# A transformer block with cross-attention: row maxima spread by turning a repeated column, and the modulation with the conditions as stationary side

## The chip, the core and the metric

The kernel runs on one core of a Trainium2 chip. The metric is the device time of one execution in microseconds. The engines are TensorE (PE in the profile, with PEld for its loads of the stationary operand), VectorE (DVE), ScalarE (ACT), GpSimd (POOL) and SyncE (SP, which here only issues transfers). A matrix product has a stationary operand, which is loaded first, and a moving one, which is streamed past it; the result lands in PSUM. A "turn" is a transpose on TensorE: the data is the stationary side and an identity matrix is streamed. An f32 product appears in the profile as two matmul instructions; an f32 turn and a bf16 matmul as one.

## The reference, cut to what matters

```python
# x (16, 224, 512), cond (16, 512), ctx (16, 750, 512), all float32; 16 heads of 32
c_proj = silu(c) @ W_mod + b_mod                      # (16, 6*512)
shift_a, scale_a, gate_a, shift_m, scale_m, gate_m = split(c_proj, 6)
x_norm = ln(x) * (1 + scale_a[:, None]) + shift_a[:, None]
q, k, v = split(x_norm @ W_qkv + b_qkv, 3)            # self-attention
x = x + gate_a[:, None] * (softmax(q k' * scale) v @ W_proj + b_proj)
q_c = ln(x) @ W_qc + b_qc                             # cross-attention
k_c, v_c = split(ln(context) @ W_kvc + b_kvc, 2)
x = x + softmax(q_c k_c' * scale) v_c @ W_cproj + b_cproj
h = gelu((ln(x) * (1 + scale_m) + shift_m) @ W_mlp1 + b_mlp1) @ W_mlp2 + b_mlp2
x = x + gate_m[:, None] * h
```

The softmax subtracts each query's largest score before the exponential. The change is about how that maximum reaches the scores in cross-attention, and about the first line, the modulation.

## The kernel before

The work runs in three stages, one after the other: self-attention (to some 760 us), cross-attention (to some 2230 us) and the MLP. Each engine works through its instructions in the order of the program; every operation is recorded through a helper at line 28, so the profile's line is L28 for nearly all of them, and one goes by tile names. Three PSUM pools serve the attention stages: `sc` for scores (one buffer of four banks), `mm` for projections and turns (three buffers of a bank) and `o` for values (one buffer of a bank).

**The opening** (lines 247 to 299). The inputs and weights are fetched by transfers on SP's and ACT's queues. ACT's queue first issues five small transfers that fill `brow`, one row of 128 for every 128 biases (line 140), then `c_in` (the conditions), then two transfers of `bg`, the gates' biases. SP's queue issues the first two 1 MB parts of W_mod (`w_mod`, two buffers), the first tokens `x` and W_qkv. ACT computes `c_act` = silu, TensorE turns it, and VectorE copies it to `c_t`, which holds the 16 conditions as columns. `brow` is turned into `bcol`, whose columns are per-partition biases; VectorE adds 1 to those of the scales and scales `bqc`. `make_part(i)` (line 279) then makes one of the six parts. A gate (parts 2 and 5) has `c_t` as stationary side and 512 columns of weights moving. A shift or scale (parts 0, 1, 3, 4) has 128 by 128 blocks of weights as stationary side and the 16 columns of `c_t` moving, 16 products of two instructions, so that the result stands with the features on the partitions; VectorE adds `bcol` and writes `mod_t`. Parts 0 and 1 come before the first turns of the normalized tokens (`xn` into `xt`, where VectorE applies `mod_t`) and the first projection. Parts 2 to 5 are put into slots of self-attention's first units by a plan (`at_slot`, line 513 on): 2 and 3 in unit 1, 4 and 5 in unit 3. A part's weights are fetched when the part two before it has been used. DMA issues wait in their queue where they need something, and so does all that is behind them on the same engine.

**A cross-attention unit** (class `Unit`, lines 960 to 1072) is one sample and four heads, 64 units in all, some 22.5 us each. Scores are computed turned, with context positions on the partitions (125) and the 224 queries along the free axis, in three rounds of two chunks (`scores`, `keep`). `keep` copies scores to `pt` (ACT) and gathers the largest over chunks in `top` (VectorE). `maxima` turns `top` (f32) so that queries stand on 112 partitions and VectorE reduces it to `mc`, 8 columns of negated maxima: four heads by two halves of the queries. `split_max(nc.gpsimd, nmc, m)` (line 122) writes each as the sum of three bf16 terms into the first three columns of `nmc`, whose other columns are zero: four POOL operations.

In the next unit, after its first round of scores, `max_row` turns the eight 112 by 128 blocks of `nmc` (bf16) into a PSUM tile of `mm`, and ACT copies that to `mrow`, rows of terms. `subtract(h)` multiplies a matrix of ones with 448 columns of `mrow`, which sums the three terms and repeats the result on 125 partitions in a tile `bc` of the pool `o`; VectorE adds it to `pt` for two heads. `subtract(0)` stands after the first slot of the round (in most units half of a projection of the keys, 375 columns), `subtract(1)` in the second round. `weights(h)` then applies the exponential (ACT) and sums over positions into `acc` (POOL). One unit later still, `values` multiplies `pt` with the values, adds sums from `acc`, and `finish` (VectorE, `at`) divides. A plan of slots lays the projections, turns, norms and fetches of the next sample between these steps. After the last unit the same steps are written out among the first MLP products (line 1105 on).

Of the kernel before, what the change touches and what calls it, by code (L numbers as in the profile page):

```python
# [8 lines left out]
F32 = mybir.dt.float32  # L9
BF16 = mybir.dt.bfloat16  # L10
# [27 lines left out]
def kernel(  # L38
# [73 lines left out]

# [6 lines left out]
    nmc = const.tile([TP, HG, TC, P], BF16, name="nmc")  # L119
    nc.gpsimd.memset(nmc, 0.0)  # L120

    def split_max(engine, nm, m):

        r = small.tile(list(m.shape), F32, name="rest")
        engine.tensor_copy(nm[:, :, :, 0], m)
        engine.tensor_tensor(r, m, nm[:, :, :, 0], ALU.subtract)
        engine.tensor_copy(nm[:, :, :, 1], r)
        engine.tensor_tensor(nm[:, :, :, 2], r, nm[:, :, :, 1], ALU.subtract)
# [9 lines left out]
    for off, vec in ((o_mod, b_mod), (o_qkv, b_qkv), (o_qc, b_qc), (o_kvc, b_kvc), (o_mlp, b_mlp1)):  # L138
        rows = vec.shape[0] // P
        nc.scalar.dma_start(out=brow[off : off + rows, :], in_=vec.rearrange("(r p) -> r p", p=P))  # L140
# [113 lines left out]
    wq, wk, wv = (load_w(ws, w_qkv[:, i * H : (i + 1) * H], f"wqkv{i}") for i in range(3))  # L254
    bg = mp.tile([B, 2, H], F32, name="bg", bufs=1)
# [4 lines left out]
    c_act = mp.tile([B, H], F32, name="c_act", bufs=1)  # L260
    nc.scalar.activation(c_act, c_in, AF.Silu)
# [7 lines left out]
    ps = ps_mm.tile([P, 512], F32, name="mm")  # L269
    turn(ps[:, :nbias], brow, ident[:nbias, :nbias])  # L270
    nc.vector.tensor_copy(bcol, ps[:, :nbias])
    for i in (1, 4):
        sl = bcol[:, o_mod + i * KC : o_mod + (i + 1) * KC]
        nc.vector.tensor_scalar(sl, sl, 1.0, None, ALU.add)

    bqc = const.tile([P, KC], F32, name="bqc")
    nc.vector.tensor_scalar(bqc, bcol[:, o_qc : o_qc + KC], SCALE, None, ALU.mult)

    def make_part(i):
        w = w_part[i]  # L280
        ps = ps_mm.tile([P, 512], F32, name="mm")
        if i % 3 == 2:
            for k in range(KC):
                mm(ps[:B, :H], c_t[:, k, :], w[:, k, :], start=(k == 0), stop=(k == KC - 1))
# [3 lines left out]
        else:  # L288
            slot = (i // 3) * 2 + i % 3
            for m in range(KC):  # L290
                for k in range(KC):
                    mm(
                        ps[:, m * B : (m + 1) * B], w[:, k, m * P : (m + 1) * P], c_t[:, k, :],
                        start=(k == 0), stop=(k == KC - 1),
                    )
# [138 lines left out]
    if True:  # L434
# [70 lines left out]
        for p in range(NP):  # L505
# [15 lines left out]
            if p == 0:  # L521
                at_slot(p, 1, 0, lambda: make_part(2))
                at_slot(p, 1, 1, lambda: make_part(3))
                at_slot(p, 1, 1, lambda: load_part(4))
                at_slot(p, 1, 1, lambda: load_part(5))
                at_slot(p, 3, 0, lambda: make_part(4))
                at_slot(p, 3, 1, lambda: make_part(5))
                at_slot(p, 3, 1, load_cross)
# [18 lines left out]
        def self_scores(p, g, j, nm):  # L547
# [15 lines left out]
            split_max(nc.vector, nm, m)  # L563
# [33 lines left out]
        make_part(0)  # L597
        make_part(1)
# [212 lines left out]
    with tc.tile_pool(name="ca", bufs=2, reuse_waits="tile") as ca:  # L811
# [152 lines left out]
        class Unit:  # L964
# [39 lines left out]
            def maxima(self):  # L1004
                m = small.tile([TP, HG, TC], F32, name="mc")
# [307 lines left out]
```

## Time and profile before

| what | value |
|---|---|
| median of 3 runs | 2943.95 us (2943.93 to 2952.13) |
| profiled execution | 2940.97 us, its span 2939.2 us |
| TensorE busy | 2850.1 us, 97% of the span |
| VectorE, ScalarE, GpSimd busy | 65%, 40%, 44% |
| mean granted TensorE clock | 0.991 |
| turns of `nmc`: 512; products of `mrow` with ones in cross-attention: 128 | mean 216 ns; 355 ns |
| ACT copies to `mrow` in cross-attention: 64 | mean 906 ns |

A row of a group reads: line, engine, operation, what it writes and reads, its shape and count; then busy time in us and mean duration in ns; then the idle time of the engine just before it and what ended most of it. For TensorE the shape is rows by columns of the stationary side, then rows by columns of the moving one. The duration of one matmul includes its way through the array, so matmuls overlap, and the distance between starts says what one takes from the stream. A row of the time order reads: start, length of a merged run of instructions, engine, operation, and in brackets the idle time before. A row of waits reads: who waited for whom, total us, how often, the longest. A row of a window reads: the window, its length, for each engine busy time and count, the granted clock as a share of full speed (unrecorded before 27 us, and then shown as 1.00), the busy share of the DMA engines and GB/s.

### The profile page before, as it was taken

To read this page: it belongs to the slowest core of one execution; us is meant where nothing else is said; L and a number is where in the kernel's file an instruction comes from. 1 tells how busy PE (TensorE), PEld (TensorE's weight loads), DVE (VectorE), ACT (ScalarE), POOL (GpSimd) and SP (SyncE) were. 2 spreads that over 40 slices of the span, in tenths; PEclk is the share of its full clock that TensorE was granted. 3 is DMA by queue.
4 is the path that set the end of the run, shared out by engine and by line. 5 is a ranking of instruction groups with operands and counts; after the bars stand their busy time and mean duration, and the time that the engine had idled before them with its cause. 6 is when DMAs were issued, how large, how long until landed. Compare 5 with 4: busy or idle time off the path is not lost.

```text
span 2939.2 us, 46558 instructions
## 1 busy us (share of the span) xinstructions
PE 2850.1 (97%) x19389; PEld 1829.9 (62%) x19389; DVE 1913.6 (65%) x2688; ACT 1175.4 (40%) x1462; POOL 1296.2 (44%) x1636
## 2 busy tenths in 40 slices
PE   8999999998999999999999999999978999999999
PEld 5544444444555565555656555555545888888888
DVE  3677766676478778777787777777775643443343
ACT  1222222221466665666566656665653022112211
POOL 1022222122367666676666766666564510221021
PEclk9999999999999999999999999999989999999999
DMA  5111110100100010100101100000012101111110
GB/s 189 59 32 32 32 32 11 59 11 26 54 32 24 22 35 24 34 28 19 34 24 34 35 18 28 26 33 24 22 44 99 55 30 49 43 47 30 54 44 29
DMA packets 55383, 114.40 MB, mean 39 GB/s; under 512 B 4308, under 2 KB 4372, under 8 KB 55172
## 3 DMA queue, kind: packets, MB, share of 16 engines
q1 hardware_dynamic: 54560, 110.58, 11.7%
q8 instruction: 152, 2.49, 0.4%
q10 hardware_dynamic: 612, 0.85, 0.1%
q14 instruction: 59, 0.48, 0.1%
HBM read 89.33 MB, written 22.09 MB: 38 GB/s over the span
## 4 chain that ended last, share of the span: by engine, by line
PE 80%; DVE 8%; issue 4%; ACT 4%; POOL 3%; DMA 1%; SPq 0%; ACTq 0%; POOLq 0%; DVEq 0%
PE mm L28 46%; PE a L28 10%; PE sc L28 9%; PE o L28 8%; PE b L28 5%; ACT pt L28 3%; PE c L28 3%; DVE at L28 2%; DVE top L28 2%; POOL acc L28 1%; DVE stats L28 1%; DVE m L28 1%; DVE mc L28 1%; ACT kt L28 1%; DMA gate<-gate_d 1%
## 5 line engine op out<-in xcount | busy, mean ns | idle before, releaser
L28 POOL TENSOR_TENSOR acc<-acc,pt 125x448 f32<-125x448 f32 x512 | 584.3, 1141 | 40.2
L28 DVE TENSOR_TENSOR pt<-pt,o 125x896 f32<-125x896 f32 x384 | 394.4, 1082 | 92.0 <-PE o L28 87.0
L28 ACT COPY pt<-sc 125x1792 f32<-125x1792 f32 x192 | 317.4, 1653 | 223.3 <-DVE top L28 199.0
L28 DVE TENSOR_TENSOR top<-top,sc 125x896 f32<-125x896 f32 x320 | 346.7, 1084 | 40.6 <-PE sc L28 34.0
L28 PE MATMUL mm<-wkvc,cxt 128*125 128x512 f32 x768 | 354.4, 604 | 8.6 <-ACT kt L28 8.6
L28 POOL TENSOR_TENSOR upd<-upd,gate 112x512 f32<-112x512 f32 (+1 forms) x60 | 78.9, 1315 | 632.5 <-DVE upd L28 627.8
L28 PE MATMUL mm<-cxt,wkvc 128*128 128x375 f32 x1024 | 350.5, 484 | 2.4 <-ACT cxt L28 2.4
L28 ACT ACTIVATE pt<-pt 125x896 f32<-125x896 f32 x384 | 339.1, 955 | 12.9 <-DVE pt L28 12.2
L28 POOL TENSOR_TENSOR acc<-pt 125x448 f32<-125x448 f32 x128 | 146.5, 1144 | 382.6 <-ACT pt L28 382.6
L28 DVE RECIPROCAL at<-o 128x224 f32<-128x224 f32 x128 | 198.8, 1553 | 102.1 <-PE o L28 102.1
L28 PEld LDWEIGHTS mm<-cxt,wkvc 128*128 128x128 f32 x1024 | 190.4, 191 | 112.7 <-issue 13.3
L28 PEld LDWEIGHTS mm<-wkvc,cxt 128*125 128x125 f32 x768 | 136.5, 187 | 175.2 <-issue 153.5
L28 ACT ACTIVATE pt<-sc 112x1792 f32<-112x1792 f32 x64 | 106.6, 1665 | 343.4 <-PE sc L28 338.8
L28 POOL TENSOR_TENSOR rstd<-mv,eps 112x2 f32<-112x2 f32 (+3 forms) x93 | 17.8, 192 | 475.5 <-DVE mv L28 475.5
L28 PE MATMUL sc<-qt,kt 32*125 32x224 f32 x3072 | 201.6, 377 | 12.9 <-ACT pt L28 12.3
L28 PE MATMUL mm<-xt,wqkv 128*128 128x448 f32 x512 | 209.0, 551 | 4.7 <-DVE xt L28 4.7
L28 DVE TENSOR_REDUCE m<-sc 112x8 f32<-112x1792 f32 x64 | 129.6, 2026 | 120.3 <-PE sc L28 120.3
L28 PEld LDWEIGHTS sc<-qt,kt 32*125 32x125 f32 x3072 | 132.9, 183 | 92.6 <-issue 41.0
L28 ACT COPY mrow<-mm 128x896 bf16<-128x896 bf16 x64 | 58.0, 906 | 309.2 <-PE mm L28 309.2
L28 PE MATMUL o<-pt,vt 125*32 125x224 f32 x3072 | 158.6, 355 | 0.0
L28 PEld LDWEIGHTS mm<-xt,wqkv 128*128 128x128 f32 x512 | 92.3, 190 | 86.7 <-issue 80.9
L28 ACT COPY mx<-a 128x512 f32<-128x512 f32 x26 | 15.3, 587 | 325.0 <-POOL upd L28 306.3
(192 smaller groups left out, 4846.7 us busy)
## 6 DMA issues: line engine op xcount, KB each, us to landing
cx<-in_ctx_dram SPq DMA_DIRECT2D x96, 250.0 KB
x<-in_x_dram SPq DMA_DIRECT2D x16, 448.0 KB
x_self<-x SPq DMA_DIRECT2D x16, 448.0 KB
x<-x_self SPq DMA_DIRECT2D x16, 448.0 KB
x_cross<-x SPq DMA_DIRECT2D x16, 448.0 KB
mx<-x_cross SPq DMA_DIRECT2D x28, 256.0 KB
w<-in_L_xcond_W_mlp_dram SPq DMA_DIRECT2D x7, 1024.0 KB
xr<-x_cross SPq DMA_DIRECT2D x28, 256.0 KB
```

The source lines that it names most:

```text
L28: return lambda *args, **kw: self.tc.keep_in_program_order(f(*args, **kw))
```

## The change

In cross-attention the split into terms, `nmc`, `max_row` and `mrow` are gone. `subtract(h)` takes each f32 column of `mc` itself as the stationary side, repeated 125 times by its access pattern (a stride of zero), and turns it: four turns of 112 columns fill the tile `bc`, which VectorE adds as before. `split_max` stays for self-attention, on VectorE.

In the modulation every part now has `c_t` as stationary side (`part_rows`), with 512 columns of weights moving. For a shift or scale ACT copies the 16 rows to SBUF, and `finish_part` turns four blocks of 16 by 128 before VectorE writes `mod_t` as before. In self-attention's plan parts 3 and 4 are finished a slot or two later than their rows are made. On ACT's queue `c_in` is issued first; the transfers of `brow` and `bg` are issued behind the activation that makes `c_act`. The turn of `brow` and the additions to `bcol` come after the rows of parts 0 and 1.

```diff
...
-    nmc = const.tile([TP, HG, TC, P], BF16, name="nmc")
-    nc.gpsimd.memset(nmc, 0.0)
-
-    def split_max(engine, nm, m):
+    def split_max(nm, m):
...
-    for off, vec in ((o_mod, b_mod), (o_qkv, b_qkv), (o_qc, b_qc), (o_kvc, b_kvc), (o_mlp, b_mlp1)):
-        rows = vec.shape[0] // P
-        nc.scalar.dma_start(out=brow[off : off + rows, :], in_=vec.rearrange("(r p) -> r p", p=P))
...
         xs[b] = load_x(sa, tokens(x, b), 6)
     load_part(1)
     wq, wk, wv = (load_w(ws, w_qkv[:, i * H : (i + 1) * H], f"wqkv{i}") for i in range(3))
+    c_act = mp.tile([B, H], F32, name="c_act", bufs=1)
+    nc.scalar.activation(c_act, c_in, AF.Silu)
+    for off, vec in ((o_mod, b_mod), (o_qkv, b_qkv), (o_qc, b_qc), (o_kvc, b_kvc), (o_mlp, b_mlp1)):
+        rows = vec.shape[0] // P
+        nc.scalar.dma_start(out=brow[off : off + rows, :], in_=vec.rearrange("(r p) -> r p", p=P))
     bg = mp.tile([B, 2, H], F32, name="bg", bufs=1)
     for i in range(2):
         lo = (2 + 3 * i) * H
         nc.scalar.dma_start(out=bg[:, i, :], in_=b_mod[lo : lo + H].partition_broadcast(B))
 
-    c_act = mp.tile([B, H], F32, name="c_act", bufs=1)
-    nc.scalar.activation(c_act, c_in, AF.Silu)
 
     c_t = mp.tile([P, KC, B], F32, name="c_t", bufs=1)
     ps = ps_mm.tile([P, 512], F32, name="mm")
...
         turn(ps[:, k * B : (k + 1) * B], c_act[:, k * P : (k + 1) * P], ident[:B, :B])
     nc.vector.tensor_copy(c_t.rearrange("p k b -> p (k b)"), ps[:, : KC * B])
 
-    ps = ps_mm.tile([P, 512], F32, name="mm")
-    turn(ps[:, :nbias], brow, ident[:nbias, :nbias])
-    nc.vector.tensor_copy(bcol, ps[:, :nbias])
-    for i in (1, 4):
-        sl = bcol[:, o_mod + i * KC : o_mod + (i + 1) * KC]
-        nc.vector.tensor_scalar(sl, sl, 1.0, None, ALU.add)
-
     bqc = const.tile([P, KC], F32, name="bqc")
-    nc.vector.tensor_scalar(bqc, bcol[:, o_qc : o_qc + KC], SCALE, None, ALU.mult)
-
-    def make_part(i):
-        w = w_part[i]
+
+    def make_columns():
         ps = ps_mm.tile([P, 512], F32, name="mm")
+        turn(ps[:, :nbias], brow, ident[:nbias, :nbias])
+        nc.vector.tensor_copy(bcol, ps[:, :nbias])
+        for i in (1, 4):
+            sl = bcol[:, o_mod + i * KC : o_mod + (i + 1) * KC]
+            nc.vector.tensor_scalar(sl, sl, 1.0, None, ALU.add)
+        nc.vector.tensor_scalar(bqc, bcol[:, o_qc : o_qc + KC], SCALE, None, ALU.mult)
+
+    def part_rows(i):
+
+        ps = ps_mm.tile([P, 512], F32, name="mm")
+        for k in range(KC):
+            mm(ps[:B, :H], c_t[:, k, :], w_part[i][:, k, :], start=(k == 0), stop=(k == KC - 1))
+        if i % 3 < 2:
+            r = mp.tile([B, H], F32, name="part", bufs=2)
+            nc.scalar.copy(r, ps[:B, :H])
+            return r
+        return ps
+
+    def finish_part(i, ps):
         if i % 3 == 2:
-            for k in range(KC):
-                mm(ps[:B, :H], c_t[:, k, :], w[:, k, :], start=(k == 0), stop=(k == KC - 1))
             g = mp.tile([B, H], F32, name="gates", bufs=1)
             nc.vector.tensor_tensor(g, ps[:B, :H], bg[:, i // 3, :], ALU.add)
             nc.sync.dma_start(out=gate_d[i // 3], in_=g)
         else:
             slot = (i // 3) * 2 + i % 3
+            rows, ps = ps, ps_mm.tile([P, 512], F32, name="mm")
             for m in range(KC):
-                for k in range(KC):
-                    mm(
-                        ps[:, m * B : (m + 1) * B], w[:, k, m * P : (m + 1) * P], c_t[:, k, :],
-                        start=(k == 0), stop=(k == KC - 1),
-                    )
+                turn(ps[:, m * B : (m + 1) * B], rows[:, m * P : (m + 1) * P], ident[:B, :B])
             for m in range(KC):
                 nc.vector.tensor_scalar(
                     mod_t[:, slot * KC + m, :], ps[:, m * B : (m + 1) * B],
...
                 for i, h in enumerate(parts):
                     at_slot(p, i // 3, i % 3 // 2, h)
             if p == 0:
-                at_slot(p, 1, 0, lambda: make_part(2))
-                at_slot(p, 1, 1, lambda: make_part(3))
+                made = {}
+
+                def part(i):
+                    made[i] = part_rows(i)
+                    if i % 3 == 2:
+                        finish_part(i, made[i])
+
+                at_slot(p, 1, 0, lambda: part(2))
+                at_slot(p, 1, 1, lambda: part(3))
                 at_slot(p, 1, 1, lambda: load_part(4))
                 at_slot(p, 1, 1, lambda: load_part(5))
-                at_slot(p, 3, 0, lambda: make_part(4))
-                at_slot(p, 3, 1, lambda: make_part(5))
+                at_slot(p, 2, 0, lambda: finish_part(3, made[3]))
+                at_slot(p, 3, 0, lambda: part(4))
+                at_slot(p, 3, 1, lambda: part(5))
+                at_slot(p, 3, 1, lambda: finish_part(4, made[4]))
                 at_slot(p, 3, 1, load_cross)
             n = p + 1
             if n < NP:
...
         norm_begin(0)
         for j in range(PB):
             norms[j].all()
-        make_part(0)
-        make_part(1)
+        rows = [part_rows(i) for i in range(2)]
+        make_columns()
+        for i in range(2):
+            finish_part(i, rows[i])
         load_part(2)
         load_part(3)
         fetch(1)
...
                 self.pts.append(pt)
 
             def maxima(self):
-                m = small.tile([TP, HG, TC], F32, name="mc")
+                self.m = m = small.tile([TP, HG, TC], F32, name="mc")
                 for h in range(2):
                     ps = ps_mm.tile([P, 512], F32, name="mm")
                     for s in range(2):
...
                         ps[:TP, : 2 * TC * CP].rearrange("p (s c t) -> p s c t", s=2, c=TC),
                         AX.X, ALU.max, negate=True,
                     )
-                split_max(nc.gpsimd, nmc, m)
-
-            def max_row(self):
-                ps = ps_mm.tile([P, 1024], BF16, name="mm")
-                for s in range(HG):
+
+            def subtract(self, h):
+
+                bc = ps_o.tile([P, 512], F32, name="o")
+                for s in range(2):
                     for c in range(TC):
+
                         lo = s * N + c * TP
-                        turn(ps[:, lo : lo + TP], nmc[:, s, c, :], ident16[:TP, :TP])
-                self.row = ca.tile([P, HG * N], BF16, name="mrow", bufs=1)
-                nc.scalar.copy(self.row, ps[:, : HG * N])
-
-            def subtract(self, h):
-
-                bc = ps_o.tile([P, 512], F32, name="o")
-                mm(
-                    bc[:CP, : 2 * N], ones16[:, :CP], self.row[:, 2 * h * N : 2 * (h + 1) * N],
-                    start=True, stop=True,
-                )
+                        col = self.m[:, 2 * h + s, c : c + 1].to_broadcast([TP, CP])
+                        turn(bc[:CP, lo : lo + TP], col, ident[:TP, :TP])
                 less = bc[:CP, : 2 * N].rearrange("p (s t) -> p s t", s=2).unsqueeze(2)
                 for pt in self.pts:
                     w4 = pt[:, 2 * h : 2 * h + 2, :].rearrange("p s (k t) -> p s k t", k=2)
...
                 last.values()
             for n in range(CH):
                 st = cur.scores(n)
-                if n == 0 and prev:
-                    prev.max_row()
                 if n == 0 and last:
                     last.finish()
                 cur.keep(n, st)
...
         sc = ps_s.tile([P, HG, 512], F32, name="sc")
         prev.values()
         mlp_plain(sc[:, 0], 0)
-        cur.max_row()
         prev.finish()
         mlp_plain(sc[:, 1], 1)
         cur.subtract(0)
```

More of the change, by code (lines that the diff above doesn't have):

```diff
@@ L117 @@
         nms.append(t)
-    nmc = const.tile([TP, HG, TC, P], BF16, name="nmc")
-    nc.gpsimd.memset(nmc, 0.0)
-    def split_max(engine, nm, m):
+    def split_max(nm, m):
         r = small.tile(list(m.shape), F32, name="rest")
[L125 to L128, printed above, removed]
+        nc.vector.tensor_copy(nm[:, :, :, 0], m)
+        nc.vector.tensor_tensor(r, m, nm[:, :, :, 0], ALU.subtract)
+        nc.vector.tensor_copy(nm[:, :, :, 1], r)
+        nc.vector.tensor_tensor(nm[:, :, :, 2], r, nm[:, :, :, 1], ALU.subtract)
     o_mod, o_qkv = 0, 6 * KC
@@ L562, in self_scores @@
             )
-            split_max(nc.vector, nm, m)
+            split_max(nm, m)
         def self_weights(p, g, j, row):
```

## The prediction

> **What bounds the kernel now.** I read the page first: busy times, slices, the chain that ended last. Then TensorE's groups, shapes kept apart, and TensorE's waits inside the cross-attention stage (760 to 2160 us). Then the order of time: one unit there, and the first 30 us. Last, windows with the granted clock.
>
> ```profile
> PE 2850.1 (97%) x19389; PEld 1829.9 (62%) x19389; DVE 1913.6 (65%) x2688; ACT 1175.4 (40%) x1462; POOL 1296.2 (44%) x1636
> PE 80%; DVE 8%; issue 4%; ACT 4%; POOL 3%; DMA 1%; SPq 0%; ACTq 0%; POOLq 0%; DVEq 0%
> ```
>
> TensorE is the bound: 97% busy, 80% of the chain. So a change is priced in two coins: start-to-start time that its matmuls take from TensorE's stream, and waits of TensorE. Work on the other engines counts only where TensorE waits for it.
>
> ```profile
> L28 PE MATMUL o<-mrow,ones 128*125 128x448 bf16 x128 | 45.4, 355 | 1.0 <-ACT mrow L28 1.0
> L28 PE MATMUL mm<-ident,nmc 112*128 112x112 bf16 x512 | 37.0, 216 | 12.0 <-POOL nmc L28 12.0
> L28 PE MATMUL mm<-ident,xn 112*128 112x112 f32 x248 | 31.0, 271 | 0.0
> PE mm L28 <- POOL nmc L28: 9.6, 15, 1.1
> ```
>
> The first two groups go away; the third is nearest to what comes. The last line, from the waits in 760 to 2160, says that 15 times TensorE stood for the split maxima on POOL; the other 2.4 of the 12.0 us is one wait at 2171 to 2174.
>
> ```profile
> 1464.93 1.04 PE L28 MATMUL sc<-qt,kt 32*125 32x224 f32 x16
> 1465.90 0.57 PE L28 MATMUL mm<-ident,nmc 112*128 112x112 bf16 x8
> 1466.30 2.75 PE L28 MATMUL mm<-cxt,wkvc 128*128 128x375 f32 x8
> 1468.90 0.35 PE L28 MATMUL o<-mrow,ones 128*125 128x448 bf16 x1
> 1469.08 2.69 PE L28 MATMUL mm<-cxt,wkvc 128*128 128x375 f32 x8
> ```
>
> Starts give the price in the stream: eight turns of nmc 0.40 us (1465.90 to 1466.30), one product with ones 0.18 (1468.90 to 1469.08).
>
> ```profile
> 3.01 0.44 ACTq L28 DMA_DIRECT2D c_in<-in_cond_dram  x1
> 8.64 0.63 ACT L28 ACTIVATE c_act<-c_in 16x512 f32<-16x512 f32 x1 [0.47 <-DMA c_in<-in_cond_dram]
> 10.30 13.84 PE L28 MATMUL mm<-c_t,w_mod 128*128 128x16 f32 x64
> 23.98 3.18 PE L28 MATMUL mm<-ident,xn 112*128 112x112 f32 x16
> 27.00 6.19 PE L28 MATMUL mm<-xt,wqkv 128*128 128x448 f32 x16
> 58.63 3.61 PE L28 MATMUL mm<-w_mod,c_t 128*16 128x512 f32 x8
> 63.37 3.70 PE L28 MATMUL mm<-c_t,w_mod 128*128 128x16 f32 x32
> ```
>
> The opening is one chain: the conditions are issued sixth on ACT's queue and land after 8 us; two parts of the modulation; the turns; the first projection at 27.00. The 64 small matmuls of two parts take 13.84 us here, but 32 of one part take 3.70 at 63.37: half speed at the start. The turns agree (16 in 3.18 us; 8 in 0.93 at 95.92). From 27.00 on matmuls have their later durations.
>
> ```profile
> 66.00:69.00 3.00, 3.00 (x38) 2.11 (x41) 1.64 (x7) 0.00 (x0) 0.25 (x2) 0.82 0.91 276
> 69.00:72.00 3.00, 3.00 (x19) 1.60 (x13) 1.54 (x1) 0.00 (x0) 2.68 (x5) 0.61 0.98 373
> ```
>
> In these windows the third number from the end is the granted clock: 0.82 and 0.61 just after part 3 (63.37 to 67.07). After part 4 (80.61) it is 0.67 and 0.76 in 84 to 90; after the gate part at 58.63 it is 1.00.
>
> **The change, part by part.**
>
> *Removed, each of 64 cross units.* Eight turns of nmc, 0.40 us, and two products with ones, 2 x 0.18: 0.77 us of TensorE's stream. ACT's mrow copy (906 ns) and four POOL operations (about 218, 206, 218, 233 ns, 1.1 us in a row) leave engines with slack: TensorE waited once, 1.0 us, for mrow.
>
> *Added, each unit.* Eight f32 turns of 112 columns with a repeated column as stationary side, four in each `subtract`. Eight xn turns took 0.93 us, one alone 0.27, so the pitch is (0.93 - 0.27) / 7 = 0.095 us: eight cost 0.76, and up to 0.83 with the hand-over at each group's end. Net -0.01 to +0.06 us a unit; I take +0.03, times 64 = +2 us. The trace shows no stationary operand with a repeated element, so from below nothing is gained, and from above its load could be dearer than the stream (third rival).
>
> Here a rule speaks against the change. The Trainium skill, "TensorE: Matmul & The Clock Gate", section on the fast weight load, has that load on for 128 weights of a type that isn't FP32. The nmc turns load so (98 ns), the new ones cannot (f32 turns of xn 147 ns). By the rule each turn would pay 49 ns more: 512 x 0.049 = +25 us. By the row the loads lie under the matmuls (pitch 0.095, below either load). I take the row.
>
> *Waits that go.* The turn needs `mc`, which VectorE reduces at the end of the unit before, and comes after a half of the keys' projection (2.6 us). So nothing takes the POOL wait's place there. At 1443.19 the scores began 1.67 us before the nmc turn instead of the 0.97 above: 0.70 lost. Fifteen times: 10.5 us. What follows in such a unit leaves room: the next scores start at 1448.99, ACT released their bank at 1447.72, so 0.70 passes and the slack is still 0.6. The wait at the end, 2.4 us, I count whole, as VectorE's next work there waits for TensorE (4.7 us, at 2178.91). Sum -13, bounds -16 and, if it is taken back, 0. POOL's freed 1.1 us a unit helps where TensorE waits for `acc` (12.6 us in all); the long ones follow other POOL work, so -1 (0 to -3).
>
> *Modulation in the loop.* Part 3 and part 4 become 8 matmuls of 512 columns like the row at 58.63: 8 x 0.43 = 3.44 us, and four turns, some 0.4, against 3.70: +0.15 each, +0.3. The ACT copy (16x512, near the 0.59 of other 512-column copies) lies under other work, since finishing waits a slot. The second effect is the clock: two stretches of 3.4 us at half speed follow the narrow matmuls, at most 1.7 us each; the gate part has the new shape and no such stretch follows it. I take -3 (0 to -3.4).
>
> *The opening.* c_in is now first on ACT's queue, brow and bg are issued behind the activation. Before, brow and c_in were issued within 3 us and c_in still took 5.6 us to land, beside the 1 MB of w_mod. I take c_in in by 3, activation, turns and c_t (0.63 + 0.58 + 0.22 and hops) by 5, so part 0 starts when w_mod is in, 6.9 by the trace, instead of 10.30. Its 8 matmuls take 3.44 us at full clock, 6.9 at half; I take 5.2, to 12.1. Part 1's weights are issued at 7.15 behind x; the DMA windows add up to 2.9 MB by 12.0 and 3.1 are needed, so it starts at 13 and ends at 17.3 (between 3.44 and 5.2). Then ACT's copy 0.6, turns 0.6, mod_t 0.66, hops 0.2: 19.4. The columns of brow (0.8 us of VectorE, early before) lie beside ACT's copy. VectorE's eight xt take 3.44 as before and pace the first projection, which ends 0.75 after them, at 23.6 instead of 30.0. That is -6.4; I take -6. Bounds: -8 (12.1 and 17.3 both earlier), and -1, if the clock stays at half up to the projection (6.9 + 13.8 + 2.5 + 3.4, and a slow projection). bg is first needed at 62, brow's columns only after part 1.
>
> The second rule bears on the clock: the same page, Part 1, says that some 3.4 us of sustained activity bring full clock whatever the spacing, and Part 4 that transposes don't count as activity. By these the 64 small matmuls would have warmed the clock by 14 us, and the shape would gain nothing. The rows say otherwise: 13.8 us of 16-column matmuls ran at half, and 3.2 us of turns ended in full clock. With the rule alone the opening gains only c_in's 3.4 us, and the two stretches nothing: 5.6 us less than I sum.
>
> **Sum:** +2 - 13 - 1 + 0.3 - 3 - 6 = -20.7, against the profiled execution's 2940.97 (span 2939.2 and 1.8 around it): 2920. The median of the three runs, 2943.95, is 3 us above that execution; on its scale I say **2923 us**.
>
> **Rivals.** *The waits move.* VectorE is 77% busy in the stage and ACT's score copies wait for it; a TensorE that comes 0.7 us earlier may stand before the next scores. For: 199 us of ACT waiting for `top`. Against: the slack of 1.2 us in the unit above. Then the 13 us stay: 2937. *The opening gives nothing.* ACT must now issue seven DMAs between the activation and the copies of the modulation's rows. Before, two bg issues of about 0.4 us spanned 3.37 us on that queue; if they stand there until the 3 MB of wqkv are in (the DMA engines are full until 24 us), the copies come at about 21 and the opening is as before: 2929. *Slower:* the repeated column. If its load reads badly, all 512 turns pay. All other terms together are -22.7, so it decides from 0.044 us a turn over 0.095; at 0.25 us a turn it costs 79 us and the time is 3000. For: the kernel itself copies a repeated column into `rep` before loading it as stationary. Against: all loads in the trace go by number of columns and type, and repeated moving operands (mrow in self-attention) run at their width.
>
> **How the numbers follow.** Forecast 0.65, waits move 0.13, opening nothing 0.13, slower 0.07, and 0.02 for anything else. 0.3% is 8.8 us, about what a measurement here can tell from no change: faster is below 2935, slower above 2953. Nearly all of the forecast, most of the second rival and a third of the first are faster: 0.79; same 0.13; slower 0.08. The range takes all gains at their ends and 3 us for clock stretches at the stage's end (-34): 2910; above, it holds the first rival and reaches 2941; the column at its worst is left out. The forecast alone lies in 2911 to 2934.
>
> **What would show it.** Right: no nmc wait among TensorE's waits and about 0.97 us from the first scores to the keys' projection in every unit; new turns at a pitch near 0.095; a first projection near 20 to 24 us; clock 1.00 in 66 to 90. Wrong: pitch over 0.14; TensorE waiting longer for `pt`; the copies of the rows held behind ACT's DMA issues; the clock at half until 27 again.

## The result, and the profile after

The changed kernel takes 2922.71 us, median of four runs (2922.62 to 2924.95), where the kernel before took 2946.26 us in four runs beside them (2943.93 to 2952.13). The ratio is 0.9922, 95% interval 0.9905 to 0.9939: faster by some 0.8%. A later measurement of the same two kernels gave 2925.01 against 2941.86 us, ratio 0.9939 (0.9927 to 0.9952), so the gain is 0.6 to 0.8%. The forecast was 2923 us. The profiled execution is 2922.65 us long with a span of 2920.9 us, 18.3 less than the span before. The forecast's sum was -20.7, so on one scale, span against span, it was 2.4 us too good. It added 3 us because the profiled execution of before lies below the median of its kernel; that of the changed kernel lies at its median. So the agreement to 0.3 us is in part luck.

The changed kernel's page, busy times and the engines' shares of the chain that ended last:

```profile
PE 2847.2 (97%) x19181; PEld 1828.9 (63%) x19181; DVE 1910.2 (65%) x2688; ACT 1119.8 (38%) x1402; POOL 1241.8 (43%) x1379
PE 83%; DVE 6%; ACT 4%; issue 4%; POOL 2%; DMA 1%; SPq 0%; POOLq 0%; ACTq 0%; DVEq 0%
```

TensorE's work is the same to 3 us, ACT and POOL each lost some 55 us. The gain is not in busy time: it is in TensorE's waits and in its clock.

The new turns among TensorE's groups, and TensorE's waits in 760 to 2160 us, both of the changed kernel:

```profile
L28 PE MATMUL o<-ident,mc 112*125 112x112 f32 x512 | 76.2, 271 | 1.2 <-DVE at L28 1.2
L28 PE MATMUL mm<-ident,cx 125*128 125x125 f32 x384 | 46.7, 270 | 0.0
```

```profile
PE mm L28 <- ACT kt L28: 7.0, 15, 0.5
PE o L28 <- POOL acc L28: 6.2, 3, 3.5
PE sc L28 <- ACT pt L28: 2.3, 1, 2.3
```

The 15 waits for `nmc`, 9.6 us, are gone, and none of that size has come up elsewhere. (The waits for `acc` are 2.8 us in this window before, but only because its edge at 2160 us cuts off one of them, which now ends at 2152; over the whole span they are four and 12.6 us before, four and 12.4 after.) Two of the waits that went, in the trace of before, the first sample's and one of thirteen alike:

```profile
778.15 0.57 PE L28 MATMUL mm<-ident,nmc 112*128 112x112 bf16 x8 [1.09 <-POOL nmc L28]
1443.19 0.57 PE L28 MATMUL mm<-ident,nmc 112*128 112x112 bf16 x8 [0.63 <-POOL nmc L28]
```

The mean of 271 ns of a new turn is its way through the array; its price is read from starts.

One unit of the changed kernel in order of time, TensorE:

```profile
1451.39 1.04 PE L28 MATMUL sc<-qt,kt 32*125 32x224 f32 x16
1452.36 2.79 PE L28 MATMUL mm<-cxt,wkvc 128*128 128x375 f32 x8
1454.99 0.59 PE L28 MATMUL o<-ident,mc 112*125 112x112 f32 x4
1455.42 2.71 PE L28 MATMUL mm<-cxt,wkvc 128*128 128x375 f32 x8
```

The keys' projection follows the first scores after 0.97 us, with no turn between. Four turns take 0.43 us from the stream (1454.99 to 1455.42), 0.107 us each.

The opening of the changed kernel, TensorE and then two rows of ACT:

```profile
6.81 6.37 PE L28 MATMUL mm<-w_mod,c_t 128*16 128x512 f32 x8 [1.48 <-DMA w_mod<-in_L_xcond_W_mod_dram]
13.49 3.61 PE L28 MATMUL mm<-w_mod,c_t 128*16 128x512 f32 x8 [0.31 <-DMA w_mod<-in_L_xcond_W_mod_dram]
17.23 0.95 PE L28 MATMUL mm<-ident,part 16*128 16x16 f32 x8
20.81 6.25 PE L28 MATMUL mm<-xt,wqkv 128*128 128x448 f32 x16 [0.22 <-PE mm L28]
...
3.98 0.63 ACT L28 ACTIVATE c_act<-c_in 16x512 f32<-16x512 f32 x1 [1.49 <-DMA c_in<-in_cond_dram]
13.22 0.57 ACT L28 COPY part<-mm 16x512 f32<-16x512 f32 x1 [8.61 <-DMA bg<-in_L_xcond_b_mod_dram]
```

The first projection starts at 20.81 instead of 27.00. Both parts wait for their weights now, so that the transfers set the first 13.5 us. Part 0 runs at half speed nearly all through, part 1 at full: 6.37 us against 3.61, and the trace's record of the clock begins with full speed at 12.4 us. (The bracket of the last row names a transfer of `bg`. ACT had issued both by 10.3 us, and the copy starts 0.04 us after part 0's last matmul ends, at 13.18: it waited for TensorE.)

Windows after parts 3 and 4 of the modulation (the third number from the end is the granted clock):

```profile
66.00:69.00 3.00, 2.18 (x28) 1.45 (x28) 2.96 (x8) 1.34 (x1) 0.00 (x0) 1.00 0.03 12
84.00:87.00 3.00, 3.00 (x26) 1.76 (x23) 1.89 (x1) 0.00 (x0) 0.00 (x0) 1.00 0.23 51
```

The two stretches at half speed that followed the narrow matmuls are gone.

To see where the 18.3 us come from, matched VectorE instructions of both traces (the reductions to maxima) are set side by side; the difference of their starts, after minus before, grows like this:

| place | difference, us | step |
|---|---|---|
| first maxima of self-attention | -6.1 | opening -6.1 |
| after part 4, and to the end of self-attention | -7.8 | -1.7 |
| first maxima of cross-attention | -7.7 | hand-over of the stages +0.1 |
| first maxima of the last sample | -17.3 | -9.6 in 15 samples |
| maxima of the last sample's third unit | -20.1 | -2.8 |
| end | -18.3 | +1.8 |

Within a sample of four units the difference moves by +0.02, 0.00, +0.14 and -0.72 us, and so again in thirteen samples. In the first, where the wait before was 1.09 us, it moves by -1.03 in that unit, and in the fifteenth, where it was 0.29, by -0.35.

### The profile page after: what moved, and what is told of

It is laid out like the page before. It is cut to its first block, busy times and chain, and to the rows that moved or that the text cites. A ratio compares the mean times of both kernels' runs of the same rounds, so it can differ in the third digit from the quotient of the medians.

```text
span 2920.9 us, 45888 instructions
## 1 busy us (share of the span) xinstructions
PE 2847.2 (97%) x19181; PEld 1828.9 (63%) x19181; DVE 1910.2 (65%) x2688; ACT 1119.8 (38%) x1402; POOL 1241.8 (43%) x1379
## 4 chain that ended last, share of the span: by engine, by line
PE 83%; DVE 6%; ACT 4%; issue 4%; POOL 2%; DMA 1%; SPq 0%; POOLq 0%; ACTq 0%; DVEq 0%
PE mm L28 45%; PE a L28 10%; PE sc L28 10%; PE o L28 10%; PE b L28 5%; ACT pt L28 3%; PE c L28 3%; DVE at L28 2%; DVE top L28 1%; POOL acc L28 1%; DVE m L28 1%; ACT kt L28 1%; DMA gate<-gate_d 1%; POOL upd L28 1%; POOL xr L28 0%
## 5 line engine op out<-in xcount | busy, mean ns | idle before, releaser
L28 PEld LDWEIGHTS mm<-cxt,wkvc 128*128 128x128 f32 x1024 | 184.4, 190 | 118.3 <-issue 17.7
L28 PE MATMUL sc<-qt,kt 32*125 32x224 f32 x3072 | 203.2, 379 | 11.7 <-ACT pt L28 11.1
L28 DVE TENSOR_REDUCE mc<-mm 112x4 f32<-112x500 f32 x128 | 80.0, 666 | 87.7 <-PE mm L28 87.7
```

The costliest lines, as they stand in the source:

```text
L28: return lambda *args, **kw: self.tc.keep_in_program_order(f(*args, **kw))
```

## The experiments

The theory is the sum of the prediction: TensorE's waits for the split maxima, the shape of the modulation's products, and the early conditions, each worth its own term and independent of the rest. The rivals are those of the prediction and some for single steps.

**The modulation alone.** The kernel before with the new opening, `part_rows` and `finish_part`, and cross-attention as it was:

```diff
-        make_part(0)
-        make_part(1)
+        rows = [part_rows(i) for i in range(2)]
+        make_columns()
+        for i in range(2):
+            finish_part(i, rows[i])
```

> The opening and the modulation as changed, cross-attention as before. Theory (the two parts add up): the first maxima of self-attention 6 us earlier, no half-speed stretch near 68 and 85 us, 7.8 us gained when cross-attention starts, and there nothing more per sample: 2933 us (2929 to 2937). Rival (what the opening gains is given back at a later wait): 2941 or more, with the gain at the start of cross-attention gone by its end.

Measured: 2937.33 us in ten runs (2933.68 to 2944.34), ratio 0.9982 (0.9972 to 0.9991), a little above the range that was expected. By matched instructions the opening gave -4.1 and the two stretches -1.7; then 4.3 us were lost again where self-attention hands over to cross-attention, and the 9.6 us of waiting for `nmc` stayed.

```profile
8.37 6.30 PE L28 MATMUL mm<-w_mod,c_t 128*16 128x512 f32 x8 [2.41 <-DMA w_mod<-in_L_xcond_W_mod_dram]
15.49 3.61 PE L28 MATMUL mm<-w_mod,c_t 128*16 128x512 f32 x8 [0.82 <-DMA w_mod<-in_L_xcond_W_mod_dram]
```

The opening has the same code as in the changed kernel, where these two rows start at 6.81 and 13.49. The weights landed 1.6 and 2.0 us later in this execution, and the projection with them. The loss at the hand-over is looked at below, with the repeated run.

**Cross-attention alone.** The kernel before with the turned column, modulation and opening as they were:

```diff
-                if n == 0 and prev:
-                    prev.max_row()
...
+                        col = self.m[:, 2 * h + s, c : c + 1].to_broadcast([TP, CP])
+                        turn(bc[:CP, lo : lo + TP], col, ident[:TP, :TP])
```

> Cross-attention as changed, the opening and the modulation as before. Theory: nothing gained at the start of cross-attention, then 0.70 us in one unit of each of the 15 samples after the first, 0.15 lost in two others, some 2.5 us at the last sample: 11 us, 2930 us (2926 to 2935). The half-speed stretches near 68 and 85 us stay. Rival (the work taken from ACT and POOL is the gain): a gain in every unit alike, some 0.3 us or more, 2920 us.

Measured: 2931.26 us (2930.55 to 2932.08), ratio 0.9961 (0.9947 to 0.9975). The difference to before is +0.5 at the first maxima of cross-attention, moves by the same +0.02, 0.00, +0.14, -0.72 per sample, and takes -2.9 in the last sample. The steps in cross-attention belong to the turned column, whatever the opening does. The two halves nearly add up: 0.9982 times 0.9961 is 0.9943. The whole change was measured at 0.9922 (0.9905 to 0.9939) and later at 0.9939 (0.9927 to 0.9952). The product lies inside the second interval and just outside the first, so nothing is shown that the two halves don't hold.

**Only the order of the queue.** `c_in` first, `brow` and `bg` behind the activation, and the narrow products of the modulation as they were:

```diff
+    c_act = mp.tile([B, H], F32, name="c_act", bufs=1)
+    nc.scalar.activation(c_act, c_in, AF.Silu)
     for off, vec in ((o_mod, b_mod), (o_qkv, b_qkv), (o_qc, b_qc), (o_kvc, b_kvc), (o_mlp, b_mlp1)):
...
-        make_part(0)
-        make_part(1)
+        made = [part_products(i) for i in range(2)]
+        make_columns()
+        for i in range(2):
+            part_add(i, made[i])
```

> Before, with c_in first on ACT's queue, brow and bg behind the activation and the columns after the products of parts 0 and 1; the modulation's matmuls stay narrow. Theory (narrow matmuls don't wake the clock): they start near 6.8 and take 13.8 us at half speed as before, so the first projection starts near 23.5 to 24 (20.8 in the changed kernel, 27.0 before), the stretches near 68 and 85 us stay: 2937 to 2939 us. Rival (any 3.4 us of steady work wakes it, so the shape adds nothing): the second part at 3.7 us, the projection near 21, 2934 us.

Measured: 2943.37 us in ten runs, ratio 0.9999 (0.9990 to 1.0009). No gain, which I had not expected. The profiled execution, 2949.55 us, is the longest of the ten.

```profile
7.87 6.98 PE L28 MATMUL mm<-c_t,w_mod 128*128 128x16 f32 x32 [1.99 <-DMA w_mod<-in_L_xcond_W_mod_dram]
15.28 7.01 PE L28 MATMUL mm<-c_t,w_mod 128*128 128x16 f32 x32 [0.42 <-DMA w_mod<-in_L_xcond_W_mod_dram]
...
22.99 3.32 PE L28 MATMUL mm<-ident,xn 112*128 112x112 f32 x16 [0.41 <-DVE bcol L28]
26.10 7.54 PE L28 MATMUL mm<-xt,wqkv 128*128 128x448 f32 x16
```

Part 0 starts 2.4 us earlier than before, but part 1 stands 0.4 us for its weights and the turns 0.4 us for the columns of `brow`; both parts take 7.0 us. The projection starts 0.9 us earlier and then takes 7.54 us instead of 6.19, as full clock came only 2.6 us into it (at 28.7 us by the trace's record, against 27.0 before). At the first maxima the kernel is 0.4 us behind the one before. So with the narrow products the earlier start bought nothing that ten runs can tell. The wide ones turn it into time: from the start of part 0 to the projection it takes 18.2 us here and 14.4 in the kernel with the modulation alone, because part 1, the small turns and the 16 turns of `xn` then run at full speed.

This run also answers the rule on the clock that the prediction set aside. The Trainium skill, "TensorE: Matmul & The Clock Gate", Part 1, has some 3.4 us of sustained activity bring full clock, whatever the spacing of the matmuls. Here 14 us of 16-column products, with a gap of 0.4 us, ran at half speed to their end (7.0 us a part, against 3.70 for part 3 before), as 13.84 us of them did before. Products of 512 columns brought full clock after some 3.1 to 5.5 us (twice what part 0 is longer than 3.61, which it takes at full clock: 5.18 to 6.37 in seven executions). For this shape the measurement decides against the rule; whether the width of the moving side or the stationary one makes the difference was not separated.

**Turns of nmc later.** The kernel before, with the eight turns of `nmc` and the ACT copy to `mrow` in the middle of the keys' projection, to take away the POOL wait without the rest of the change:

```diff
+                if k == 1 and hf == 0 and between:
+                    between.pop()()
...
-                    prev.max_row()
+                    if (b, g) == units[-1]:
+                        prev.max_row()
+                    else:
+                        between.append(prev.max_row)
```

> Before, with the eight turns of nmc and ACT's copy of mrow put into the middle of the keys' projection, so that POOL's split has 1.3 us more; no work is removed. Theory (the gain in cross-attention is the wait): no wait for nmc, 0.70 us gained once in a sample, 10 to 12 us in all, 2930 to 2933 us. Rival (the gain comes of removed work): within 3 us of before, 2941 to 2945.

Measured: 3163.68 us, ratio 1.0755 (1.0739 to 1.0771); I had expected a gain. TensorE and then ACT in one unit:

```profile
1442.15 1.49 PE L28 MATMUL mm<-cxt,wkvc 128*128 128x375 f32 x4
1446.50 0.35 PE L28 MATMUL o<-mrow,ones 128*125 128x448 bf16 x1 [2.86 <-ACT mrow L28]
...
1443.99 1.65 ACT L28 COPY pt<-sc 125x1792 f32<-125x1792 f32 x1 [6.70 <-DVE top L28]
1445.54 0.91 ACT L28 COPY mrow<-mm 128x896 bf16<-128x896 bf16 x1
```

The nmc wait fell to 1.3 us, as meant. But ACT's copy to `mrow` now stands behind its copy of the scores, which itself waits for VectorE's `top`, and TensorE waits for `mrow`: 163 us in all. Units are 2.4 to 4.6 us longer, some by more than the wait itself: the clock falls in many of these gaps (the mean granted clock is 0.968). So the wait could not be had by moving the turns to this place, the only one tried: the chain runs from VectorE over POOL, TensorE and ACT back to TensorE, and what POOL gained there ACT lost. The change takes POOL and ACT out of it.

**VectorE earlier.** The kernel before, one statistic of the context's norm moved from just ahead of the late maxima to an earlier slot:

```diff
-                            b, 1 + 2 * hf, (4, 5, 5)[c] - hf, lambda b=b, hf=hf, c=c: cnorms[b + 2, hf].stats(c)
+                            b, 1 + 2 * hf, ((2, 5, 5), (3, 4, 4))[hf][c], lambda b=b, hf=hf, c=c: cnorms[b + 2, hf].stats(c)
```

> Before, with one statistic of the context norm in cross-attention's second unit of a sample moved two rounds ahead, to where VectorE stands idle 1.3 us; mc is then ready 0.9 us earlier and POOL's split too. No work is removed. Theory (what cross-attention gains is the wait for nmc): the 0.70 us of one unit in each of some 13 samples go, 9 us, 2933 us (2931 to 2936 where the clock's stretches are as before). Rival (the removed work matters): within 2 us of before.

Measured: 2940.72 us in ten runs, ratio 0.9989 (0.9980 to 0.9998), where 2933 was expected. TensorE's waits in 770 to 2150, then POOL in the unit that waits:

```profile
PE mm L28 <- POOL nmc L28: 5.2, 15, 1.1
```

```profile
1434.82 4.80 POOL L28 TENSOR_TENSOR acc<-acc,pt 125x448 f32<-125x448 f32 x4
1439.58 1.27 POOL L28 TENSOR_TENSOR x<-x,upd 112x512 f32<-112x512 f32 x1
1440.79 0.22 POOL L28 CAST nmc<-mc 112x8 bf16<-112x8 f32 x1
```

The maxima are 0.79 us earlier, but the wait in such a unit shrank only by 0.34, from 0.63 to 0.29, and each sample by 0.33. POOL stood idle for 0.28 us ahead of the split before; now it comes from its sums and an addition to `x`, one behind the other, and starts the split at 1440.79. So the wait had two feeders, VectorE's statistics and POOL's own queue, and serving the first gave about half of it. The prediction named the split on POOL; the queue ahead of it is the part it did not see. The turned column makes both irrelevant. That a wait shortened by 0.34 shortens the sample by 0.33 shows besides that these waits were on the path one for one.

**Each turn twice.** The changed kernel, every new turn issued twice into the same place:

```diff
-                        turn(bc[:CP, lo : lo + TP], col, ident[:TP, :TP])
+                        for _ in range(2):
+                            turn(bc[:CP, lo : lo + TP], col, ident[:TP, :TP])
```

> The changed kernel with each turn of mc issued twice, the same output. Theory (a turn costs its 0.107 us in TensorE's stream, nothing hides it): 512 x 0.107 = 55 us more, 2970 to 2980 us. Rival (turns lie in TensorE's waits): under 2945 us.

Measured: 2967.55 us (two runs, 2964.46 and 2970.65), ratio 1.0080 (1.0062 to 1.0099), 45 us over the changed kernel, where the theory gave 55. TensorE in one unit:

```profile
1457.75 1.02 PE L28 MATMUL o<-ident,mc 112*125 112x112 f32 x8
1458.62 2.71 PE L28 MATMUL mm<-cxt,wkvc 128*128 128x375 f32 x8
```

Eight turns take 0.87 us of the stream, 0.109 each. Three units of a sample grow by that, 0.87; the fourth only by 0.15, so that the mean over a sample is 2.77 / 32 = 0.087 us. In that unit 0.72 us of added work goes unseen: TensorE had time to give there, among others in its waits for `kt` (15, 7.0 us in the changed kernel), which are gone from this trace. The rival (turns hidden altogether) is out: the turns cost, as much as the prediction's row or a little more.

**A plain stationary side.** The changed kernel with an ordinary tile of zeros in place of the repeated column, which leaves the subtraction of the maxima out:

```diff
-                        col = self.m[:, 2 * h + s, c : c + 1].to_broadcast([TP, CP])
+                        col = flat[:, 2 * s + c, :]
```

> The changed kernel with an unrepeated f32 tile of zeros as stationary side of the turns in cross-attention, so the maxima are left out there. Theory (loads lie under the stream): loads of 0.14 to 0.15 us instead of 0.188, the same start-to-start distance of the turns, within 2 us of the changed kernel, 2921 to 2925 us. Rival (a repeated column costs its longer load): 0.041 x 512 = 21 us less, 2902 us.

Measured: 2923.19 us (2922.04 to 2924.62), ratio 0.9928 (0.9913 to 0.9943): no difference to the repeated column. Its load, and two starts:

```profile
L28 PEld LDWEIGHTS o<-ident,flat 112*125 112x125 f32 x512 | 74.8, 189 | 41.1 <-issue 25.3 <-PE mm L28 0.3
```

```profile
1456.76 0.59 PE L28 MATMUL o<-ident,flat 112*125 112x112 f32 x4
1457.18 2.71 PE L28 MATMUL mm<-cxt,wkvc 128*128 128x375 f32 x8
```

A plain tile loads in 189 ns, as long as the repeated column (189 ns in the changed kernel), and four turns take 0.42 us. The repetition costs nothing that shows, and the expected load of 0.14 to 0.15 us was wrong. The load is longer than that of the `xn` turns (141 ns) for another reason, which no run here shows, and it lies under the stream: the distance between starts is 0.105 to 0.107 us.

**The last unit earlier.** The changed kernel, in the last unit the subtraction and the weights issued one plain MLP product earlier, since the changed kernel's longest wait is now there:

```diff
         prev.finish()
-        mlp_plain(sc[:, 1], 1)
         cur.subtract(0)
         cur.weights(0)
-        mlp_plain(sc[:, 2], 2)
+        mlp_plain(sc[:, 1], 1)
         cur.subtract(1)
         cur.weights(1)
+        mlp_plain(sc[:, 2], 2)
```

> The changed kernel with the last unit's two subtractions each moved ahead of one MLP product; before the change the copy to mrow needed that product as cover, now nothing does. Theory: the last unit's exponentials and sums begin 3.5 us earlier and TensorE's 6.2 us wait for acc there shrinks to some 3: 2919.5 us (2917 to 2922). Rival (the clock's windows or VectorE take it back): 2922 to 2925 us.

Measured: 2919.81 us (2919.60 to 2922.73), ratio 0.9921 (0.9908 to 0.9933). TensorE's longest wait from 2193 us on, first of the changed kernel, then of this one:

```profile
PE o L28 <- POOL acc L28: 6.2, 1, 6.2
```

```profile
PE o L28 <- POOL acc L28: 2.4, 1, 2.4
```

The wait for the last sums is 3.8 us shorter, and the median 2.9 us below the changed kernel's first four runs, as expected. It is the better of the two kernels by a little: its ratio to before overlaps with that of the changed kernel, so the gain rests on the wait in the trace, on the medians (2922.71 and 2925.01 for the changed kernel, 2919.81 here), and on the next experiment, which has this edit too and whose five runs all lie below the five of the changed kernel repeated beside them.

**The tail on ScalarE.** That kernel, with the modulations of the first MLP group of the last unit (24 instructions in the trace) on ScalarE instead of VectorE:

```diff
+        if on_act:
+            nc.scalar.activation(
+                dst, psum_ap, AF.Identity, bias=mod_t[:, i_shift + k, b : b + 1],
+                scale=mod_t[:, i_scale + k, b : b + 1],
+            )
+            return
```

> The changed kernel with the last sample's subtraction and weights issued one plain product earlier, and the 16 modulations of the first MLP group of the last unit computed on ScalarE instead of VectorE. Theory (in the last sample the plain products wait for VectorE to hand over the accumulators, and for ScalarE's weights only because of that): TensorE's wait for pt in the tail (8.8 us in the changed kernel) shrinks by half, 3 to 5 us less than the earlier kernel with only the moved subtraction: 2915 to 2918. Rival (ScalarE is what is late there): the modulations push the exponents back, 2921 or more.

Measured: 2919.40 us (2917.44 to 2922.17), ratio 0.9920 (0.9907 to 0.9934): nothing beyond the earlier subtraction. TensorE's waits in 2130 to 2260:

```profile
PE sc L28 <- ACT pt L28: 10.9, 4, 3.5
...
PE mm L28 <- ACT mxt L28: 2.3, 1, 2.3
```

The wait for `pt` in that window stays (11.1 before the edit), and TensorE now waits 2.3 us for ScalarE's modulations as well. The theory is wrong: ScalarE is late there by itself, or waits for something other than VectorE's modulations.

**The changed kernel again.** Nothing edited.

> The changed kernel itself once more, with nothing edited, to see what one execution differs from another by. Theory (a few us of any comparison are where the transfers of the opening land and how the half-speed stretches of the clock fall on the hand-over from the self-attention to the cross-attention, and have nothing to do with the code): the steps of the cross-attention repeat to 0.1 us (+0.13, -0.70, +0.02 and 0 per sample of four units against before), while the opening differs by up to 2 us from the -6.1 and the hand-over by up to 3 us; median 2921 to 2925. Rival (each step is the code's own): opening and hand-over repeat to 0.2 us as well.

Measured: 2925.01 us in five runs (2923.83 to 2926.29), ratio 0.9939 (0.9927 to 0.9952). The steps per sample repeat to 0.02 us: +0.02, 0.00, +0.14, -0.72; from the fourth unit to the last one of the fifteenth sample they sum to -7.5 in both profiles. The opening is -5.3 instead of -6.1, and the hand-over of the stages +2.4 instead of +0.1. So the rival is out: opening and hand-over are not the code's alone. The granted clock at the hand-over, in the first profile of the changed kernel and then in this one:

```profile
700.00:705.00 5.00, 2.29 (x30) 1.31 (x33) 4.44 (x9) 1.66 (x1) 0.00 (x0) 0.69 0.33 102
705.00:710.00 5.00, 3.95 (x44) 1.96 (x36) 2.53 (x3) 0.97 (x1) 0.00 (x0) 0.63 0.00 0
710.00:715.00 5.00, 4.09 (x27) 1.65 (x28) 3.04 (x3) 0.69 (x1) 0.00 (x0) 0.72 0.01 3
715.00:720.00 5.00, 5.00 (x12) 2.08 (x11) 0.69 (x1) 0.00 (x0) 1.32 (x2) 0.94 0.00 0
```

```profile
700.00:705.00 5.00, 1.37 (x23) 0.92 (x22) 4.78 (x9) 1.66 (x1) 0.00 (x0) 0.86 0.46 138
705.00:710.00 5.00, 4.51 (x44) 2.28 (x44) 3.02 (x3) 0.41 (x1) 0.00 (x0) 0.50 0.00 0
710.00:715.00 5.00, 3.70 (x26) 1.74 (x27) 2.25 (x2) 1.25 (x1) 0.00 (x0) 0.50 0.01 3
715.00:720.00 5.00, 5.00 (x10) 1.86 (x10) 1.48 (x3) 0.00 (x0) 0.00 (x0) 0.77 0.00 0
```

The same code in the same place gets a mean of (0.69 + 0.63 + 0.72 + 0.94) / 4 = 0.75 of the clock in one execution and 0.66 in the other.

## Why the prediction was right, point by point

| step of the prediction | forecast, us | measured, us |
|---|---|---|
| turns for `nmc` and the products with ones | +2 | +2.0 (+0.16 per sample of four units) |
| POOL waits of 15 samples | -10.5 | -10.7 (-1.03, thirteen times -0.72, -0.35) |
| POOL wait at the end | -2.4 | -2.8 |
| waits for `acc` | -1 | 0 |
| modulation in the loop, and the two stretches | +0.3 and -3 | -1.7 together |
| opening | -6 | -6.1, and -4.1 to -6.3 over seven executions |
| not forecast | | -0.9, then +1.8 and +0.1 |

- **The turns.** The sum was right and its parts were not. A new turn takes 0.107 to 0.109 us, not the 0.095 of the `xn` row, so that eight cost 0.86 to 0.87, beyond the 0.83 at the upper end. What they replace took 0.40 + 2 x 0.18 = 0.76 (the prediction has 0.77), so a unit should have lost 0.1 us and a sample 0.4. What pays for it was not looked for: f32 turns that follow the new ones are cheaper. Twelve turns of `cx` take 1.38 us behind them (1440.27 to 1441.65) against 1.50 behind a product with ones before (1453.68 to 1455.18), twice in a sample, and the group's busy time fell to 46.7 us, from 50.4. That the waits for `kt` fell from 8.6 to 7.0 us gives another 0.1 a sample. The unrepeated tile and the doubled turns show that neither the rule of the fast weight load (+25 us) nor the rival of the repeated column applies: loads of 189 ns stay under the stream, and the price stayed below the 0.139 us from which the column would decide. The prediction's reading that all loads go by number of columns and type does not hold: f32 loads of 128 columns take 141 ns for the turns of `cx` and 190 for the products.
- **The waits.** As forecast: TensorE's time comes 1:1 where the wait was, in one unit of four, and nothing took its place; the slack of 1.2 us that was read from one unit held in the others. The rival "the waits move" is out by the steps of both kernels with the turned column and by the waits above.
- **The waits for `acc`** did not shrink (12.6 us before, 12.4 after, four each): POOL's freed time came where it was not late.
- **The stretches of half speed.** The mechanism is right, both went, but together with the modulation's matmuls they were worth 1.7, not 2.7. Each gave 1.2 (the matched differences go from -6.1 to -7.3 and from -6.6 to -7.8), where 1.5 was taken. Between the two, 0.8 is lost again, as TensorE now waits for VectorE:

```profile
68.59 3.27 PE L28 MATMUL mm<-xt,wqkv 128*128 128x448 f32 x8 [0.82 <-DVE qk L28]
```

This wait stands in all seven profiled executions with the wide products (0.81 or 0.82 us each) and not in the trace of before. The four turns of part 3 now take one of the three buffers of `mm`, so by the order of the tiles the projection behind them needs the buffer that VectorE's copy to `qk` frees, at 68.54; no run tested this. The prediction priced these turns by their time on TensorE alone, and put what they do to the buffers at nothing.

- **The opening.** Right in sum. Start of part 0 (6.81, forecast 6.9) and of part 1 (13.49, forecast 13) were as worked out; part 0 needed 6.37 instead of the middle value of 5.2, which cost nothing, since part 1 stood for its weights until 13.49 anyway. The rival "the opening gives nothing" is out: ACT's copy of the first rows starts at 13.22, within 0.1 us of the end of part 0, and not behind the issues of `bg`. The prediction put -6 down to both edits of the opening without saying which one carries it: alone, the order of the queue gave nothing that could be told.
- **Not forecast.** A stretch at half speed near 805 us, in the first sample of cross-attention, is missing in the changed kernel (-0.9). In the repeated execution it is there (at 799 us), and where only the modulation was changed it is missing too, so the execution has a part in it. But four of the five traces with the split maxima have it and only one of the seven with the turned column; whether the change makes it rarer stays open. At the end 1.8 us were given back. There the changed kernel ran at half speed in a whole window:

```profile
2180.00:2190.00 10.00, 5.29 (x40) 4.06 (x40) 9.96 (x20) 6.17 (x6) 5.67 (x5) 0.50 0.01 2
```

In the repeated execution the last part gave -0.9 instead of +1.8, but that is the exception. Between the maxima of the third and the fourth unit of the last sample, 1.2 to 1.8 us are lost in six of the seven profiled executions with the turned column, and at most 0.1 in the four further ones with the split maxima. So this loss mostly goes with the change; why is not shown. The hand-over of the first profile (+0.1) was lucky: in eight executions whose opening was edited it cost 0.1 to 4.3 us, 1.3 or more in seven of them, against 0.5 at most in the three that left all of self-attention as it was. The prediction had no term for either place. It came out near the sum because one of them fell out well and the stretch near 805 us was missing.

## What to carry to other kernels

Where an engine is 97% busy, look for the one unit in which it waits and ask which engines the awaited value passes through: taking two engines out of that chain gave the whole wait back, while serving one of its feeders earlier gave half and moving the consumer cost 220 us. Count added turns at the distance between starts of the very place where they will stand, look at the instructions behind them, which may become cheaper, and count the buffers that they take as well as their time. Price a moved transfer or an earlier start together with what it lets run: alone, an earlier start of narrow matmuls at half clock bought nothing.

## What the hardware showed that was not expected

The stretches at half speed have lengths of 3.4 us and its multiples (3.4, 6.8, 13.7, 20.5 us in these traces), and begin at another place in each execution (the first one near 700 us between 696.4 and 703.6 in the seven with the wide products). Where the work thins out, at the hand-over near 700 us, matched instructions lost between -0.1 and 4.3 us more than in the first profile of before, over eleven executions; the most is over a third of what the turned column brings in the cross-attention. The Trainium skill, "TensorE: Matmul & The Clock Gate", Part 1, has this window of some 3.4 us run freely, which these lengths agree with; its price at such a place comes from these runs. The landing of the first weights varies by another 1.6 us (6.81 to 8.37 for the start of part 0). The first can be larger than four of the six terms of the sum, the second than two, and where such terms matter, matched instructions inside one stage tell them apart and the total time doesn't.
